# Order of two side jobs in one stage: unpacking of weights first, tables of heads 32 to 47 second

## The chip, the cores and the metric

One core of one Trainium2 chip. The metric is the device time of one execution in microseconds (us); the shown time of the kernel before is the median of three runs. The core's engines are TensorE (PE, matmuls, and PEld, its weight loads), VectorE (DVE), ScalarE (ACT), GpSimd (POOL) and SyncE (SP, which here only issues DMAs). Each engine works through its own instructions strictly in program order and waits on semaphores for the others.

## The reference

```python
def _L0_cond_ref(u, length, log_dt, C, log_A_real, A_imag, D):
    mask = (jnp.arange(Lq) < length[:, None]).astype(u.dtype)
    u_m = u * mask[:, None, :]
    kernel = _get_kernel(log_dt, C, log_A_real, A_imag, Lq)      # [64 heads, 1024]
    k_f, u_f = jnp.fft.rfft(kernel, n=2 * Lq), jnp.fft.rfft(u_m, n=2 * Lq)
    y = jnp.fft.irfft(u_f * k_f, n=2 * Lq)[..., :Lq] + u_m * D[:, None]
    return y * mask[:, None, :]

def _L0_ffn_ref(x, ...):
    x2 = x.reshape(-1, H).astype(jnp.float32)
    Wg, Wu, Wd = (dequant_gptq(...) for gate, up, down)          # 4-bit weights, groups of 128 rows
    gate, up = x2 @ Wg, x2 @ Wu
    inter = gate * jax.nn.sigmoid(gate) * up
    return (inter @ Wd).astype(jnp.float16).reshape(B, S, H)

x = x + _L0_ffn_ref(_L0_cond_ref(x, ...), ...)                   # x: (32, 64, 1024) float32
```

A long convolution of length 1024 for each of 64 heads (its kernel is made from the parameters of a state space model), then a gated feed-forward layer of 1024 by 2752 with packed 4-bit weights, then the residual sum. The 32 x 64 rows of `x` are the tokens.

## The kernel before

The 2048 tokens are worked on as four blocks of 512: block b holds the heads 16b to 16b+15, for all 32 batch entries. Activations are held as a high and a low float16 half (`xh`, `xl`, `ihl`), so each product is two matmuls.

The convolution of a head (`conv_head`) multiplies by Toeplitz tiles. To get them, a head's kernel is first computed from tables: `head_coefficients`, a decay table (Exp on ACT, L179), phase tables (`phase_tables`: L192 to L204 on DVE, Sin and Square on ACT, L207 and L209), and two factors (`kernel_factors`, L218 to L223 on DVE). `make_kernel` multiplies the factors on PE (L427), splits the result (L431, L433) and writes it to DRAM (`kpad`, L435); `toeplitz` (L529) reads it back as a 128 x 2 x 1024 tile.

A weight piece is made by the generator `unpack`, in three steps that lie apart in the program: SP issues two loads (packed bytes, L582, and zero points, L583); after a pause DVE shifts and masks the nibbles in place (L588) and POOL adds the zero points in two or fewer cuts (L594); after another pause DVE subtracts 64 and turns bytes into fp8, cut by cut (L603). `drain` runs the 34 pieces in order, each beginning its loads while an earlier one is worked on: 22 pieces of the gate and up weights (`gu`, in tiles `w` and `wmix`), then 12 of the down weights (`dn`, tiles `wd`, three parts for each of four pairs of output tiles).

The feed-forward layer runs in chains. A chain (`gu_one`, `gu_pair`, `dn_pair`) accumulates in PSUM over the groups of 128 input rows. Since each group has its own scale, the accumulator is rescaled after every group by the ratio of neighbouring scales: by DVE (L622, one instruction for 128 x 1024 values) or by ACT (L624), whichever a plan of the engines' times says is done earlier. Up to three chains are in flight, so that PE works on two while the third is rescaled. Four matmuls make one group of one chain.

The function `roll` orders all this. Its items come in stages: 0 and 1 (first four weight tiles for block 0 and for block 1, each alone), 2 (**the two-block stage**: the other gate and up tiles, blocks 0 and 1 together, 35 chains; two extra items make the kernels of heads 32 to 39 and 40 to 47), 3 and 4 (down, blocks 0 and 1), 5 (gate and up for blocks 2 and 3), 6 and 7 (down, blocks 2 and 3). After each step of a chain `roll` serves the side jobs of the current stage in the order of their list in `sides`. Each job earns credit at its rate; a job with `None` in third place spends all its credit, one generator step for each unit, but only while `c.room()` holds, that is, while the plan has DVE no more than 1200 ns and ACT no more than 1500 ns behind PE. A step that gives DVE work moves that plan on, and so can close the room to the job behind it in the list.

What isn't ready in time is forced: `need`, called where a chain begins (and at groups 0, 8 and 16 of a down chain), runs the unpacking, pauses left out, until the piece is there; `kernel_item` does the same with `third`, the generator of the tables of heads 32 to 47. The tile framework then fixes the instruction order of each engine.

Stage 3 has as side jobs the unpacking, the tables and kernels of heads 48 to 63 (`fourth`) and the convolutions of blocks 2 and 3 (`convs`).

Of the kernel before, what the change touches and what calls it, by code (L numbers as in the profile page):

```python
# [32 lines left out]
RATES = {"first": (0.5, 4.6), "fill": (1.0, 0.8), "third": 0.5, "late": 0.5, "convs": 1.9}  # L33
# [819 lines left out]
def tile_ssm_ffn(ctx, tc, io):  # L853
# [4 lines left out]
    def drain(gens):  # L858
        for u, ahead in zip(gens, gens[2:] + [None, None]):
            for n, _ in enumerate(u):  # L860
                if n == 1 and ahead is not None:
                    next(ahead)
                yield

    unpacks = [c.unpack_gu(i) for i in (*range(NI - 1), NI, NI - 1)] + [Later(c.unpack_dn, k, part) for part in range(3) for k in range(4)]
    unpack_it = c.unpacking = drain(unpacks)
# [123 lines left out]
    def third():  # L990
        tiles = [c.cv.tile([128, 2, L], F16, name="t0", bufs=3) for _ in range(3)]
        small = [c.cv.tile([128, 8, 4, B], F16, name=k) for k in ("uh", "ul", "uh", "ul")]
        take = c.scratch(tiles[:2])
        c.prm = take([128, 5, H], F32)
        nc.sync.dma_start(c.prm, io["prm"])
        for _ in range(4):
            yield
        coefficients = head_coefficients(nc, nc.vector, co, take, c.prm, c.cst[:, 66:67], 32, 32)
        while True:
            with c.after("dve"), c.after("act"):  # L1000
                if next(coefficients, "end") == "end":
                    break
            c.dve(1000)
            yield
        yield from c.decays(c.scratch(tiles[2:]), (32, 40))
        c.small = ScratchPool(c.scratch(small))
        c.taps(c.small, 32)
        for h0 in (32, 40):
            yield from c.tables(ScratchPool(c.scratch(tiles[:2])), h0, 8)
            yield from c.factors(c.small, h0, 8, c.xds[h0])  # L1010

    third_it = third()
# [37 lines left out]
    def residuals():  # L1050
# [7 lines left out]
    sides = {  # L1058
        0: [(unpack_it, RATES["first"][0], None), (group_it, 1.0, None), (second_it, RATES["first"][1], True)],
        1: [(unpack_it, RATES["fill"][0], None), (third_it, RATES["fill"][1], None)],  # L1060
        2: [(third_it, RATES["third"], None), (unpack_it, RATES["fill"][0], None)],
        3: [(unpack_it, RATES["fill"][0], None), (fourth_it, RATES["late"], False), (convs_it, RATES["convs"], False)],
        4: [(fourth_it, RATES["fill"][1], None), (convs_it, RATES["convs"], True)],
        6: [(residuals(), 1.0, True)],
# [80 lines left out]
```

## Time and profile before

| what | value |
|---|---|
| median of three runs | 1068.9 us (1068.55 to 1068.94) |
| profiled execution, its own time | 1069.55 us |
| its span in the profile | 1067.8 us |
| PE busy | 1019.1 us, 95% |
| DVE busy | 804.4 us, 75% |
| ACT busy | 777.6 us, 73% |
| POOL busy | 248.4 us, 23% |
| mean granted PE clock | 0.993 |
| first matmul of the two-block stage, of the down stage of block 0, of stage 5 | about 138, 395 and 572 us |

The span is the time from the first to the last instruction of the profiled execution; the execution's own time is a little longer. A line of a group in the profile names source line, engine, operation, output and inputs, shape and count, then the busy time and the mean of one in ns, then how long the engine sat idle before such instructions and what ended that. In a timeline each line has start and length in us, and in brackets the idle time of that engine just before, with the instruction that ended it; equal instructions that follow each other are merged (x2). A row of windows has, after its length, busy time and number of instructions for PE, PEld, DVE, ACT and POOL, then the granted PE clock, the DMA share and GB/s. Matmuls overlap in the pipeline, so a matmul of 0.38 us can follow the one before after 0.22 us.

### The profile page before, as it was taken

Reading aid. Unit: us, or ns where it says so; the run is one execution under the profiler, and the core shown is the slowest. Engines: PE = TensorE matmul, PEld = TensorE weight load, DVE = VectorE, ACT = ScalarE, POOL = GpSimd, SP = SyncE. Lnnn points to the kernel's source line nnn. Section 1 sums busy time; section 2 is a strip of 40 time slices with the busy share of each in tenths; the row PEclk is TensorE's granted clock in tenths of the full one; section 3 lists DMA queues with packets and bytes.
Section 4 is the critical chain, followed back from the end, with each engine's and each line's share of the span. In section 5 each row is a group of like instructions: output and inputs, shape, how many; then the busy total and the mean of one; then the engine's idle time right before and its main releaser. Section 6 shows DMA issues by size and latency. Waiting matters only on the chain.

```text
span 1067.8 us, 15316 instructions
## 1 busy us (share of the span) xinstructions
PE 1019.1 (95%) x5824; PEld 508.8 (48%) x5824; DVE 804.4 (75%) x924; ACT 777.6 (73%) x1033; POOL 248.4 (23%) x270
## 2 busy tenths in 40 slices
PE   2979999999899999999999999999999999999996
PEld 2857444444344445555565444444444444444442
DVE  8765788888987787886556767777787777777776
ACT  4867678787677778777777776666666667778775
POOL 0433133232332352223012102222211122102102
PEclk9989999999999999999999999999999999999999
DMA  6976321111011422568663001000000002424002
GB/s 203 316 238 216 107 79 40 40 60 40 32 57 51 140 91 104 165 178 273 183 206 119 30 20 39 21 21 20 12 20 21 20 21 61 147 80 155 33 1 79
DMA packets 52066, 99.74 MB, mean 93 GB/s; under 512 B 9492, under 2 KB 11412, under 8 KB 51992
## 3 DMA queue, kind: packets, MB, share of 16 engines
q1 hardware_dynamic: 38888, 70.09, 20.6%
q0 software_dynamic: 5280, 17.31, 4.3%
q10 hardware_dynamic: 7824, 11.37, 3.7%
q8 instruction: 45, 0.74, 0.3%
q14 instruction: 29, 0.24, 0.1%
HBM read 78.99 MB, written 19.76 MB: 92 GB/s over the span
## 4 chain that ended last, share of the span: by engine, by line
PE 80%; DVE 9%; ACT 4%; issue 3%; DMA 2%; POOL 1%; DVEq 0%; SPq 0%; ACTq 0%; POOLq 0%
PE chq L691 22%; PE chq L692 22%; PE chq L746 13%; PE chq L747 12%; PE cq L552 6%; PE chq L669 2%; PE chq L668 2%; DVE chq L622 1%; DMA t<-kpad 1%; ACT chq L624 1%; DVE v L704 1%; ACT chq L644 1%; DVE chq L641 1%; ACT sg L699 1%; PE chq L751 1%
## 5 line engine op out<-in xcount | busy, mean ns | idle before, releaser
L691 PE MATMUL chq<-xh,w 128*128 128x512 f16 x1216 | 459.6, 379 | 7.3 <-DVE chq L622 2.1
L692 PE MATMUL chq<-xl,w 128*128 128x512 f16 x1216 | 457.0, 379 | 0.0
L622 DVE TENSOR_SCALAR chq<-chq,gur 128x1024 f32<-128x1024 f32 x261 | 332.5, 1289 | 96.0 <-PE chq L692 95.4
L624 ACT ACTIVATE chq<-chq,gur 128x1024 f32<-128x1024 f32 x285 | 303.7, 1085 | 89.0 <-PE chq L692 88.4
L644 ACT ACTIVATE chq<-chq,dnr 128x512 f32<-128x512 f32 x374 | 242.7, 661 | 74.3 <-PE chq L747 68.1
L746 PE MATMUL chq<-ihl,wd 128*128 128x512 f16 x672 | 253.7, 379 | 2.2 <-DVE wd L603 0.8
L747 PE MATMUL chq<-ihl,wd 128*128 128x512 f16 x672 | 253.2, 379 | 0.0
L641 DVE TENSOR_TENSOR chq<-chq,dnr 128x1024 f32<-128x1024 f32 x128 | 156.5, 1231 | 77.5 <-PE chq L747 77.0
L692 PEld LDWEIGHTS <-w 128*128 128x128 fp8e4 x1216 | 118.5, 97 | 155.8 <-issue 20.4
L691 PEld LDWEIGHTS <-w 128*128 128x128 fp8e4 x1216 | 118.3, 97 | 147.9 <-issue 2.0
L310 POOL TENSOR_TENSOR ihl<-v,ihl 128x512 f16<-128x512 f32 x42 | 48.3, 1149 | 344.4 <-ACT ihl L633 344.4
L747 PEld LDWEIGHTS <-wd 128*128 128x128 fp8e4 x672 | 65.5, 97 | 71.2 <-issue 6.2
L746 PEld LDWEIGHTS <-wd 128*128 128x128 fp8e4 x672 | 65.4, 97 | 69.1 <-DVE wd L603 2.0
L552 PEld LDWEIGHTS <-t 128*128 128x128 f16 x1152 | 81.4, 98 | 34.2 <-DMA t<-kpad 1.3
L552 PE MATMUL cq<-uh,t 128*128 128x256 f16 (+3 forms) x720 | 91.3, 228 | 0.4 <-DMA t<-kpad 0.4
L552 PE MATMUL cq<-ul,t 128*128 128x256 f16 (+3 forms) x360 | 72.2, 228 | 0.0
L569 POOL TENSOR_TENSOR xl<-y,xh 128x512 f16<-128x512 f32 x28 | 36.4, 1298 | 145.1 <-ACT xh L567 142.7
L633 ACT CAST ihl<-v 128x512 f16<-128x512 f32 x42 | 25.9, 616 | 56.5 <-DVE v L704 53.1
L704 DVE SCALAR_TENSOR_TENSOR v<-chq,gul,sg 128x1024 f32<-128x1024 f32 x38 | 48.6, 1280 | 16.7 <-PE chq L692 7.9
L668 PE MATMUL chq<-xh,w 128*128 128x512 f16 x128 | 48.8, 384 | 4.5 <-ACT xh L567 3.1
L644 ACT ACTIVATE chq<-chq,gur 128x512 f32<-128x512 f32 x66 | 43.2, 660 | 13.6 <-PE chq L669 12.4
L310 POOL TENSOR_TENSOR spill<-v,spill 128x512 f16<-128x512 f32 x42 | 48.7, 1160 | 14.3 <-ACT spill L633 14.3
(258 smaller groups left out, 799.0 us busy)
## 6 DMA issues: line engine op xcount, KB each, us to landing
t<-kpad SPq DMA_DIRECT2D x48, 512.0 KB, 4.8
spill<-spill POOLq DMA_DIRECT2D x42, 256.0 KB, 2.3
ihl<-spill ACTq DMA_DIRECT2D x42, 256.0 KB, 2.7
z<-zc SPq DMA_DIRECT2D x29, 256.0 KB, 4.2
u<-xF SPq DMA_DIRECT2D x12, 512.0 KB, 4.4
xr<-xT SPq DMA_DIRECT2D x12, 512.0 KB, 4.7
out<-xr POOLq DMA_DIRECT2D x24, 256.0 KB, 2.9
w<-qgu SPq DMA_DIRECT2D x21, 256.0 KB, 4.0
```

What stands on the lines that cost most here:

```text
L310: self.nc.gpsimd.tensor_tensor(out, a, b, op)
L552: nc.tensor.matmul(q[:, d:, h % 2, :], t0[:, lw, 128 * d:128 * d + 128], uu[:, 0:8 - d, h % 4, :], start=(d == 0 and k == 0 and h % 2 == 0 ...
L622: self.mark("dve", self.nc.vector.tensor_scalar(q, q, col, None, ALU.mult))
L624: self.mark("act", self.nc.scalar.activation(q, q, AF.Copy, scale=col))
L641: self.mark("dve", self.nc.vector.tensor_tensor(q, q, cols.to_broadcast([128, 2, 512]), ALU.mult))
L644: self.mark("act", self.nc.scalar.activation(q[:, k], q[:, k], AF.Copy, scale=cols[:, k]))
L668: nc.tensor.matmul(q[:, k], lw, xh[:, g, :], start=(g == 0), stop=False, skip_group_check=True)
L691: nc.tensor.matmul(q[:, b], lw, xh[:, g, :], start=(g == 0), stop=False, skip_group_check=True)
L692: nc.tensor.matmul(q[:, b], lw, xl[:, g, :], start=False, stop=(g == GH - 1), skip_group_check=True)
L704: nc.vector.scalar_tensor_tensor(v, q, last, self.sg.pop(ct - 21), ALU.mult, ALU.mult)
L746: nc.tensor.matmul(qs[j], lw, self.ihl[:, g, 0], start=(g == 0), stop=False, skip_group_check=True)
L747: nc.tensor.matmul(qs[j], lw, self.ihl[:, g, 1], start=False, stop=False, skip_group_check=True)
```

## The change

In the two-block stage the list of side jobs is turned round. `unpack_it` is served first at every step, at its rate of 1.0, and `third_it` second, at its rate of 0.5; before it was the other way. Rates, conditions and all other stages stay.

```diff
@@ sides @@
         1: [(unpack_it, RATES["fill"][0], None), (third_it, RATES["fill"][1], None)],
-        2: [(third_it, RATES["third"], None), (unpack_it, RATES["fill"][0], None)],
+        2: [(unpack_it, RATES["fill"][0], None), (third_it, RATES["third"], None)],
         3: [(unpack_it, RATES["fill"][0], None), (fourth_it, RATES["late"], False), (convs_it, RATES["convs"], False)],
```

In the built program this moves the unpacking of all later pieces forward: the last L603 of weight tile 12, for example, stands 93 matmuls ahead of its first use before and 239 after, and the loads of the last down piece are issued in the two-block stage. The tables move back: the decay table from matmul place 1345 to 1562, the first factors' end from 1576 to 1866, the second's from 1732 to 2093. Places count PE's matmuls in program order; the two-block stage has the places 1038 to 2182, block 0's down stage begins at 2183. The numbers of matmuls and of unpacking steps are the same in both; the plan, which sees another order, also gives a few rescales to the other engine (of the two-block stage's L622 two fewer, of its L624 two more).

## The prediction

> **What bounds the kernel now.** I read the page first. TensorE (PE) is busy for 95% of the span and holds 80% of the chain of work that ended last; VectorE (DVE) and ScalarE (ACT) are busy for three quarters each, mostly with the rescales that stand between two matmul groups of one chain.
>
> ```profile
> PE 1019.1 (95%) x5824; PEld 508.8 (48%) x5824; DVE 804.4 (75%) x924; ACT 777.6 (73%) x1033; POOL 248.4 (23%) x270
> PE 80%; DVE 9%; ACT 4%; issue 3%; DMA 2%; POOL 1%; DVEq 0%; SPq 0%; ACTq 0%; POOLq 0%
> L622 DVE TENSOR_SCALAR chq<-chq,gur 128x1024 f32<-128x1024 f32 x261 | 332.5, 1289 | 96.0 <-PE chq L692 95.4
> ```
>
> Only waits of PE count, then. Next, the windows by stage: the two-block stage ends at about 395 us, the first down stage at about 490, the second at about 572.
>
> ```profile
> 195.00:395.00 200.00, 195.12 (x913) 86.00 (x911) 164.07 (x174) 151.70 (x164) 63.98 (x71) 1.00 0.21 67
> 395.00:490.00 95.00, 91.58 (x699) 53.09 (x697) 79.83 (x100) 73.07 (x114) 29.91 (x35) 1.00 0.49 155
> 490.00:572.00 82.00, 81.99 (x655) 49.96 (x654) 42.33 (x41) 63.68 (x101) 15.60 (x16) 1.00 0.65 204
> ```
>
> The columns are length, then PE, weight loads, DVE, ACT, POOL, clock and DMA. PE's clock is 1.00, so nothing here is the clock. PE's worst stretch is in the timeline of PE, and beside it that of DVE:
>
> ```profile
> 282.99 0.38 PE L692 MATMUL chq<-xl,w 128*128 128x512 f16 x1
> 284.89 0.38 PE L691 MATMUL chq<-xh,w 128*128 128x512 f16 x1 [1.52 <-DVE chq L622]
> ...
> 286.18 0.38 PE L691 MATMUL chq<-xh,w 128*128 128x512 f16 x1 [0.48 <-issue]
> ...
> 287.78 0.38 PE L691 MATMUL chq<-xh,w 128*128 128x512 f16 x1 [0.58 <-DVE w L603]
> ...
> 291.50 0.39 PE L691 MATMUL chq<-xh,w 128*128 128x512 f16 x1 [0.29 <-DVE w L603]
> ```
>
> ```profile
> 284.75 2.89 DVE L603 TENSOR_SCALAR w<-w 128x1024 fp8e4<-128x1024 uint8 x2
> 287.56 1.28 DVE L622 TENSOR_SCALAR chq<-chq,gur 128x1024 f32<-128x1024 f32 x1
> 288.75 0.86 DVE L588 TENSOR_SCALAR w<-w,cst 128x1024 uint16<-128x1024 uint16 x2
> 290.24 2.34 DVE L603 TENSOR_SCALAR w<-w 128x1024 fp8e4<-128x1024 uint8 x2 [0.62 <-POOL w L594]
> ```
>
> The weights of tiles 14 and 15 are unpacked at the last moment: DVE makes them (L588, L603) while PE stands before their first matmul, and the rescales (L622) queue behind. The down stage has the same picture:
>
> ```profile
> 471.15 0.39 PE L746 MATMUL chq<-ihl,wd 128*128 128x512 f16 x1 [0.63 <-DVE wd L603]
> ```
>
> ```profile
> 483.67 0.59 PE L751 MATMUL chq<-ic,wd 128*128 128x512 f16 x2 [1.31 <-DVE chq L641]
> ```
>
> **The measure of a loss.** Undisturbed wide matmuls start 0.216 us apart (282.78, then 282.99). What a start is later than that is lost to PE for good. I call matmuls by their place in PE's program order. First uses stand within 26 places of each other in the two programs, so places stand for time. A rescale that has waited starts 0.42 us after its last matmul's start, so 0.2 after that matmul's slot (the hop below); back to back on DVE it takes 1.2 of its 1.29 us, L603 0.6 of 0.68.
>
> **That the order does change.** In the built programs the last L603 of tile 13 stands 2 matmuls ahead of its first use before, 224 after; tile 14: 1 and 242; tile 15: 6 and 230; tile 17: 3 and 235. The down pieces that stood 2, 1, 8 ahead of, or behind, their use stand 379 to 452 ahead. From L603's 0.68 us and the loads' 3.7 to 4.9 us of landing, 200 matmuls (43 us) hide any of them. Nothing differs after place 3525 (572 us).
>
> **Removed in the two-block stage.** Losses at 259.24 (0.49), 284.89 (1.68), 286.18 (0.64), 287.78 (0.75), 291.50 (0.45), 293.83 (0.16) and 318.54 (0.15): 4.3 us, all at a first use or behind such a burst on DVE. Bounds: 2.5 (the 1.68 stays, as a rescale can be late for other reasons) to 4.3. I take 4.3, since in the new order no unpacking stands next to a first use.
>
> **Removed in the down stage.** Directly behind L603: 439.64 (0.32), 457.87 (0.26), 464.38 (0.31), 471.15 (0.79): 1.7. Behind DVE's queue: 442.84 (0.35), 469.93 (0.26), 483.67 (1.48): 2.1. Nine L603, five L588 and ten POOL adds (L594) leave this stage; the queue before 483.67 is a residual add (1.65 us), table work and a split, which partly stay. I take 1.0 of the 2.1. Sum 2.7, bounds 1.7 to 3.8.
>
> **Added to the two-block stage.** Those nine L603 and five L588: 9 x 0.683 + 5 x 0.475 = 8.5 us of DVE. Cover: DVE sits idle for 200 - 164 = 36 us of the window. Their weight loads (5 more there) go out on SP ahead of the three Toeplitz loads (L529), which land in 4.8 us and are first used at place 2207, 100 matmuls (21 us) behind. Without that cover a load would cost its 4.8 us. Where the cover is thin, I add up places:
>
> - The decay table's Exp moves from place 1345 to 1562, and the next Silu stands at 1572: two table loads around one Exp. From place 1540 ACT and DVE owe: 0.2 hop, Silu 1.1, product on DVE 1.2, two casts 1.2, a rescale 1.1, load 1.28, Exp 1.06, load 1.28, Silu 1.1 = 9.5 us. PE needs that bank at place 1579, 39 x 0.216 = 8.4 us on. So 1.1 late; the old Silu load's loss at 225.39 (0.32) goes. Net +0.8, bounds -0.3 (all hidden, as the old Exp's load at 208.31 was) and +1.6.
>
> ```profile
> 208.31 1.28 ACT L179 ACT_TABLE_LOAD   x1
> 222.93 1.28 ACT L699 ACT_TABLE_LOAD   x1
> ```
>
> - The factors of heads 40 to 47 (L218 to L223), formerly ended at place 1732, now end at 2093, three places ahead of the matmuls (2096) that read them: `kernel_item` had to force them. From place 2074 DVE owes: hop and product 1.4; then a rescale that waits for PE 2081 (1.73), done at 3.2, while PE wants it at 2086 (2.6): 0.6 late; L218 and L219 0.35 each and a rescale 1.2, done at 5.1, wanted at 4.1: 1.0 late; L222, L603, L223 1.4, done at 6.5, wanted at 6.4: 0.1. Together 1.7; the trace of before loses 0.3 there. Net +1.4. What waits behind is all of PE. Bounds 0 and 3.3 (five factor steps at 0.42 by their rows, 2.1, and a whole rescale, 1.2, all uncovered).
> - The phase tables of heads 32 to 39 cost 1.37 before (229.72 to 241.50: 0.23, 0.25, 0.56, 0.33), those of 40 to 47 0.1. Now L603, L588, L194, L197, L198 and a rescale queue at places 1685 to 1709: 5.2 to 6.0 us against 5.2, some 0.7 late; the second set, at places 1952 to 1970, some 0.5 by the same count. Net -0.3, bounds -1.5 (all hidden) to +0.7 (both 1.1). L194 ranges widely by its row:
>
> ```profile
> L194 DVE TENSOR_TENSOR t<-wl,cst x2: 681/1060/1439, 229.6 to 262.8; 128x512 f32<-128x512 f32 x2
> L603 DVE TENSOR_SCALAR w<-w x36: 679/683/1639, 72.5 to 357.3; 128x1024 fp8e4<-128x1024 uint8 x36
> ```
>
> - Places 2000 to 2105: by the rows' durations DVE owes 22.7 us there, against 17.0 before and PE's 21.4. Overlap of back-to-back instructions hides some, waiting for PE adds some. Beyond the second bullet I take +0.8, the middle of 0 and 1.5 (a little over 22.7 - 21.4).
>
> Two rules of the Trainium skill speak against the change. "ScalarE: Activation LUTs", section "Table sets: the hidden batching unit", wants functions of one set batched and gives about 2.7 us for a load; this trace has 1.283 us each time, and the trace decides. By the page's figure the first bullet would be 2.8 us dearer. "SBUF — State Buffer", section "Who interferes with whom", says that VectorE instructions with two SBUF inputs and some single-input ones block against GpSimd; the two rows above (0.68 to 1.44, 0.68 to 1.64) are as if it were so. If three more of them met L594, the sum by this rule would lose some 2.5 us of DVE time, most of it under the idle 36.
>
> **The sum.** -4.3 - 2.7 + 0.8 + 1.4 - 0.3 + 0.8 = -4.3 us. The profiled span of 1067.8 (its own time 1069.55, 0.65 above the median of 1068.9) becomes 1063.5; the median becomes 1064.6. With the terms' nearer bounds the likeliest case runs from 1062.3 to 1066.7.
>
> **Rivals.**
>
> - The moved work is nearly free. For it: DVE's 36 idle us, and that the planner gives rescales to ACT when DVE is full. Against it: the factors stand directly before their matmuls. All of 4.3 + 3.8 gone, 0.9 lost: -7.2, 1061.7. Chance 0.15.
> - The stall moves. The high bounds 1.6 + 3.3 + 0.7 + 1.5 = 7.1 give back the 7.0. For it: PE waits in order, so the factors and the Exp block all three chains. Against it: each high bound needs the worst overlap. 1069.0, no change. Chance 0.17.
> - Slower: DVE becomes the bound of the two-block stage from place 1565 to 2105. The 8.5 us come on top in full, only the down stage's 2.7 are won: +5.8, 1074.7. It decides once DVE's work exceeds PE's pace over long stretches and not only over the last 105 places. Against it: by rows the stretches between 1571 and 2000 hold 12 to 14.5 us of DVE against PE's 13.8 per 64 places. Chance 0.07.
> - That the edit does nothing is excluded by the order told above.
>
> **Numbers.** The forecast has 0.61. Two times apart by less than 0.2% (2.1 us: 1066.8 to 1071.0) cannot be told from no change here. Faster: 0.15 and nearly all of 0.61, 0.74; the same: 0.18; slower: 0.08. The range, 1061.6 to 1068.6, takes in most of the forecast, of the first rival and half of the second.
>
> **What would show it.** Right: no PE wait on L603 between 195 and 490 us; PE's waits by DVE near 440 to 484 us mostly gone; two table loads within 4 us near 256, with a wait of about 1 us behind them; a wait near 372 us on L622 and L223. Wrong: DVE above 95% busy in the second half of the stage, or PE waiting more than 3 us before the matmuls of L427 at place 2096, or fresh waits of ACT's rescales around the tables' Sin and Square.

## The result, and the profile after

| | before | after |
|---|---|---|
| median | 1070.04 us (1068.55 to 1072.18, 11 runs) | 1073.45 us (1071.24 to 1076.07, 11 runs) |
| ratio | 1 | 1.0034, 95% interval 1.0025 to 1.0043 |
| span of the profiled execution | 1067.8 us | 1073.2 us |
| PE's places 1038 to 2182, two-block stage | 257.0 us | 265.6 us |
| places 2183 to 2862, first down stage | 94.8 us | 91.9 us |
| before place 1038; from place 2863 on | 138.3; 577.7 us | 137.8; 577.9 us |

The kernel became 0.34% slower (3.4 us), where 0.4% faster (4.3 us) was forecast. The forecast was made from the first three of the eleven runs of before, whose median is 1068.9 us. The down stage gains 2.9 us, about what was forecast; the two-block stage loses 8.6 us. The page of after, as far as it answers to the lines of before:

```profile
PE 1019.6 (95%) x5824; PEld 511.1 (48%) x5824; DVE 809.4 (75%) x925; ACT 775.9 (72%) x1029; POOL 247.2 (23%) x270
PE 79%; DVE 11%; ACT 4%; issue 3%; DMA 2%; POOL 0%; DVEq 0%; SPq 0%; ACTq 0%
L622 DVE TENSOR_SCALAR chq<-chq,gur 128x1024 f32<-128x1024 f32 x259 | 330.6, 1290 | 91.8 <-PE chq L692 90.4
```

DVE's busy time rises by 5.0 us with one instruction more, and its share of the chain of work that ended last from 9 to 11%. The windows of after, for the two-block stage and the two down stages (columns as in the prediction):

```profile
138.00:403.00 265.00, 251.53 (x1162) 111.59 (x1161) 223.19 (x278) 197.93 (x217) 89.22 (x102) 0.99 0.21 67
403.00:495.00 92.00, 90.72 (x695) 53.10 (x693) 73.50 (x89) 69.67 (x107) 22.15 (x25) 1.00 0.43 139
495.00:578.00 83.00, 82.92 (x671) 50.74 (x671) 42.26 (x41) 64.23 (x102) 16.00 (x15) 1.00 0.64 206
```

DVE is busy for 223 of 265 us: 84%, so it isn't the bound over the stage. It is late at single places. PE's losses by place (start to start, less the pitch of an undisturbed matmul, us), summed from the two traces (a sum can be off by 0.1 to 0.2, and in the last row by more, with the pitch that is taken):

| places | before | after | what is lost there after |
|---|---|---|---|
| 1038 to 1189 | 2.6 | 4.0 | 1.71 at place 1080 (before 0.33): ACT waits for the landing of a store |
| 1190 to 1339 | 0.8 | 2.8 | 1.13 and 1.16 at 1196 and 1334: stretched table steps and L603, L588 ahead of a rescale |
| 1340 to 1559 | 2.2 | 1.6 | the phase tables' four losses are gone, 0.54 is new |
| 1560 to 1589 | 0.5 | 1.8 | 1.33 behind the Exp between two table loads |
| 1590 to 1719 | 4.1 | 1.0 | the forced weights' losses are gone |
| 1720 to 1859 | 0.7 | 2.6 | 0.92, 0.73, 0.32, 0.32 from 1828 to 1852 |
| 1860 to 1989 | 1.0 | 2.1 | 1.29 at 1957 |
| 1990 to 2065 | 0.0 | 0.2 | |
| 2066 to 2105 | 0.3 | 4.9 | the factors of heads 40 to 47 |
| 2106 to 2183 | 0.5 | 0.1 | |
| 2184 to 2862 | 6.9 | 3.8 | the late down pieces are gone |

Place 1080 is no work of the change: instructions stand alike there, and e2 below, which has after's order up to there, loses 0.41. What differs is how long the store takes from issue to landing: 2.58 us in before, 2.65 in e2, 3.96 in after, and 3.94 in the trace of e5, which loses 1.69 there.

**The dearest place.** The timelines of after, first PE, then DVE, then POOL:

```profile
382.78 0.44 PE L691 MATMUL chq<-xh,wmix 128*128 128x512 f16 x1 [2.51 <-DVE chq L622]
383.01 0.63 PE L691 MATMUL chq<-xh,w 128*128 128x512 f16 x1
383.43 0.63 PE L692 MATMUL chq<-xl,w 128*128 128x512 f16 x1
```

```profile
377.90 1.29 DVE L622 TENSOR_SCALAR chq<-chq,gur 128x1024 f32<-128x1024 f32 x1 [0.28 <-PE chq L692]
379.10 1.13 DVE L218 SCALAR_TENSOR_TENSOR ul<-t,t 128x256 f32<-128x256 f32 x1
380.15 1.37 DVE L219 SCALAR_TENSOR_TENSOR uh<-t,ab 128x256 f32<-128x256 f32 x1
381.44 1.28 DVE L622 TENSOR_SCALAR chq<-chq,gur 128x1024 f32<-128x1024 f32 x1
```

```profile
378.79 1.16 POOL L310 TENSOR_TENSOR ihl<-v,ihl 128x512 f16<-128x512 f32 x1 [1.36 <-ACT ihl L633]
379.91 1.33 POOL L310 TENSOR_TENSOR spill<-v,spill 128x512 f16<-128x512 f32 x1
```

PE stands for 2.51 us until the rescale of 381.44 is done. Two factor steps stand before that rescale. They take 1.13 and 1.37 us, where 0.41 and 0.42 are usual (the row of e6 below), and for just that time POOL makes the low halves of the products (L310, a subtraction with both inputs in SBUF). Then the matmuls start 0.43 us apart, not 0.216. The windows of after at this place show why:

```profile
380.00:382.00 2.00, 0.27 (x2) 0.00 (x0) 2.00 (x3) 1.09 (x1) 1.70 (x2) 1.00 0.00 0
382.00:384.00 2.00, 1.22 (x4) 0.53 (x4) 2.00 (x5) 0.00 (x0) 0.10 (x1) 0.74 0.36 135
384.00:386.00 2.00, 2.00 (x18) 0.89 (x17) 0.59 (x1) 0.98 (x1) 0.00 (x0) 0.50 0.72 219
386.00:388.00 2.00, 2.00 (x17) 1.09 (x15) 0.45 (x2) 1.54 (x4) 0.00 (x0) 0.91 0.92 225
```

The granted clock (last column but two) fell to 0.50, by the records from 382.96 to 386.38 us. The stall so costs some 1.3 us more after its end.

**The same in small** at 316 to 323 us: PE, DVE and POOL of after.

```profile
320.78 0.38 PE L691 MATMUL chq<-xh,w 128*128 128x512 f16 x1 [0.75 <-DVE chq L622]
...
322.37 0.38 PE L691 MATMUL chq<-xh,w 128*128 128x512 f16 x1 [0.56 <-DVE chq L622]
```

```profile
316.63 2.89 DVE L603 TENSOR_SCALAR wd<-wd 128x1024 fp8e4<-128x1024 uint8 x2
319.45 1.28 DVE L622 TENSOR_SCALAR chq<-chq,gur 128x1024 f32<-128x1024 f32 x1
```

```profile
316.27 1.15 POOL L310 TENSOR_TENSOR ihl<-v,ihl 128x512 f16<-128x512 f32 x1 [2.15 <-ACT ihl L633]
317.38 1.60 POOL L310 TENSOR_TENSOR spill<-v,spill 128x512 f16<-128x512 f32 x1
```

Two L603 that usually need 1.3 us back to back take 2.89 beside POOL, and the rescale behind them starts 1.6 us late. Nothing was forced here; the piece has over 300 matmuls of slack. The rows by line over the whole of after (shortest, median, longest in ns) tell which instructions stretch and which never do:

```profile
L603 DVE TENSOR_SCALAR wd<-wd x24: 411/684/1641, 316.6 to 452.9; 128x1024 fp8e4<-128x1024 uint8 x20, 128x512 fp8e4<-128x512 uint8 x4
L588 DVE TENSOR_SCALAR wd<-wd,cst x12: 406/477/1374, 307.2 to 423.9; 128x1024 uint16<-128x1024 uint16 x8, 128x768 uint16<-128x768 uint16 x4
L622 DVE TENSOR_SCALAR chq<-chq,gur x259: 1277/1293/1295, 141.6 to 917.0; 128x1024 f32<-128x1024 f32 x130
```

The rescales (PSUM in, PSUM out) take the same time throughout this trace. What lies in SBUF stretches, in these two rows up to threefold. Counted over DVE's instructions of the two-block stage that are over 150 ns above the shortest of their shape, the stretch is 11.4 us in 19 instructions before and 18.7 us in 31 after: 7.3 us more, made of 6.4 more beside the adds of the unpacking (L594), 2.3 more beside L310 and 1.4 less beside POOL's products for the decay table (L175). In the down stage it falls from 6.5 to 3.2 us.

### The profile page after: what moved, and what is told of

The parts are those of the page before. It is cut to its first block, busy times and chain, and to the rows that moved or that the text cites. A ratio compares the mean times of both kernels' runs of the same rounds, so it can differ in the third digit from the quotient of the medians.

```text
span 1073.2 us, 15317 instructions
## 1 busy us (share of the span) xinstructions
PE 1019.6 (95%) x5824; PEld 511.1 (48%) x5824; DVE 809.4 (75%) x925; ACT 775.9 (72%) x1029; POOL 247.2 (23%) x270
## 4 chain that ended last, share of the span: by engine, by line
PE 79%; DVE 11%; ACT 4%; issue 3%; DMA 2%; POOL 0%; DVEq 0%; SPq 0%; ACTq 0%
PE chq L691 21%; PE chq L692 20%; PE chq L746 13%; PE chq L747 13%; PE cq L552 6%; DVE chq L622 3%; PE chq L669 2%; PE chq L668 2%; DMA t<-kpad 1%; ACT chq L624 1%; ACT chq L644 1%; DVE v L704 1%; ACT sg L699 1%; PE chq L751 1%; DVE w L603 0%
## 5 line engine op out<-in xcount | busy, mean ns | idle before, releaser
L691 PE MATMUL chq<-xh,w 128*128 128x512 f16 x1216 | 459.2, 379 | 12.1 <-DVE chq L622 6.2
L692 PE MATMUL chq<-xl,w 128*128 128x512 f16 x1216 | 457.4, 379 | 0.0
L622 DVE TENSOR_SCALAR chq<-chq,gur 128x1024 f32<-128x1024 f32 x259 | 330.6, 1290 | 91.8 <-PE chq L692 90.4
L624 ACT ACTIVATE chq<-chq,gur 128x1024 f32<-128x1024 f32 x287 | 305.7, 1085 | 91.5 <-PE chq L692 91.2
L644 ACT ACTIVATE chq<-chq,dnr 128x512 f32<-128x512 f32 x368 | 239.3, 661 | 74.8 <-PE chq L747 68.8
L641 DVE TENSOR_TENSOR chq<-chq,dnr 128x1024 f32<-128x1024 f32 x131 | 160.4, 1231 | 81.4 <-PE chq L747 80.7
L692 PEld LDWEIGHTS <-w 128*128 128x128 fp8e4 x1216 | 118.8, 98 | 163.6 <-issue 28.4
L691 PEld LDWEIGHTS <-w 128*128 128x128 fp8e4 x1216 | 118.8, 98 | 146.5 <-issue 3.6
L310 POOL TENSOR_TENSOR ihl<-v,ihl 128x512 f16<-128x512 f32 x42 | 48.3, 1150 | 307.0 <-ACT ihl L633 307.0
L310 POOL TENSOR_TENSOR spill<-v,spill 128x512 f16<-128x512 f32 x42 | 49.4, 1177 | 15.7 <-ACT spill L633 15.7
```

The source lines that it names most:

```text
L310: self.nc.gpsimd.tensor_tensor(out, a, b, op)
L622: self.mark("dve", self.nc.vector.tensor_scalar(q, q, col, None, ALU.mult))
L624: self.mark("act", self.nc.scalar.activation(q, q, AF.Copy, scale=col))
L641: self.mark("dve", self.nc.vector.tensor_tensor(q, q, cols.to_broadcast([128, 2, 512]), ALU.mult))
L644: self.mark("act", self.nc.scalar.activation(q[:, k], q[:, k], AF.Copy, scale=cols[:, k]))
L691: nc.tensor.matmul(q[:, b], lw, xh[:, g, :], start=(g == 0), stop=False, skip_group_check=True)
```

## The experiments

In the expectations these theories stand by letters. J: the factors are made just in time, and the stalls are those of work that comes too late. P: work of DVE in SBUF is stretched beside POOL's, and the rescales queue behind it. L: the 8.5 us of unpacking that moved into the stage are too much for DVE. C: the half clock behind PE's idle time is a large part of the loss.

**e1, the tables at full rate.** In after, the tables' credit doubled:

```diff
-RATES = {"first": (0.5, 4.6), "fill": (1.0, 0.8), "third": 0.5, "late": 0.5, "convs": 1.9}
+RATES = {"first": (0.5, 4.6), "fill": (1.0, 0.8), "third": 1.0, "late": 0.5, "convs": 1.9}
```

> The changed kernel with the tables' rate at 1.0 in place of 0.5: weights still first, but the factors of heads 40 to 47 end at place 1973, 109 ahead of their matmuls, and are not forced. Theory J (the just-in-time factors at places 2066 to 2105 cost most: 4.9 us lost there in the changed kernel's trace, with 3.4 us of half clock, against 0.3 before): that loss falls below 1 us, and the time is 4 to 5 us below the changed kernel, 1068.5 to 1069.5, no slower than before. Theory P (side work on DVE is stretched beside POOL's subtractions and adds, 18.7 us in the two-block stage against 11.4, and rescales queue behind it): the stretch stays at 16 us or more, single losses of 1 us stay, the time is 1070 to 1072. Theory L (8.5 us more DVE work in the stage is what costs): no better than the changed kernel, 1072 to 1074.

Measured: 1071.51 us, ratio to before 1.0013 (1.0003 to 1.0022), span 1068.6. The last factors now end at place 1973, and places 2066 to 2105 lose 0.3 us. Larger losses stand elsewhere: 2.08 at 1593, 2.20 at 1708 (0.53 in after), 1.16 at 1842; the 1.28 at 1957 stays as in after. In time is not enough; DVE's stretch in the stage is 19.2 us. The 2.20 at 1708 is only in part stretch. There DVE stands still, with a rescale behind, until POOL has done the add that an L603 needs:

```profile
292.29 1.20 DVE L603 TENSOR_SCALAR w<-w 128x1024 fp8e4<-128x1024 uint8 x1 [1.46 <-POOL w L594]
```

In after no instruction of DVE in this stage waits so for POOL behind 144.4 us. The time, 1071.5, is as theory P had it; theory J's part, the loss at the factors, went as it said and didn't bring the time.

**e2, the kernels of heads 40 to 47 two chains later.** In after:

```diff
-            for at, h0 in ((33, 40), (29, 32)):
+            for at, h0 in ((35, 40), (29, 32)):
```

> The changed kernel with the item that makes the kernels of heads 40 to 47 two chains later in the list: its matmuls stand at place 2178 and the factors end at 2110, 68 places ahead. All other orders stay. Theory J: the loss of 4.9 us at places 2066 to 2105 goes, PE's clock stays at 1.00, time 1068.5 to 1069.5. Theory P: losses of 1 us elsewhere stay; as the L218 and L219 stand beside POOL's subtractions still, 1 us of the 4.9 stays: 1070 to 1071. Theory L: 1072 or more.

Measured: 1069.61 us, ratio 0.9997 (0.9988 to 1.0006): before's time. Places 2066 to 2105 lose 0.25 us, all other losses of after stay to within 0.2 us (1.12 and 0.97 at 1196 and 1334, 1.33 at 1576, 2.3 from 1828 to 1852, 1.29 at 1957), save that of place 1080. Two losses are new, 0.59 and 0.42 at 2107 and 2118. The 1 us that theory P left at the factors didn't stay. The windows of e2 around the place:

```profile
372.00:382.00 10.00, 9.92 (x47) 4.39 (x46) 9.02 (x11) 7.34 (x9) 4.83 (x6) 1.00 0.19 67
382.00:400.00 18.00, 17.32 (x94) 7.95 (x93) 15.85 (x18) 12.63 (x14) 6.82 (x8) 1.00 0.28 85
```

DVE is as full as in after (224.2 us busy between 138 and 399 us, where after has 223.2 between 138 and 403), and the clock stays at 1.00. So this one place is worth 1073.45 - 1069.61 = 3.8 us of after's median, more than the 3.4 by which after is slower. And the rest of the change together is worth nothing: its gains pay for its other losses.

**e3 and e9, the weights of the two-block stage first, then the tables, the down pieces last.** In after, the job is split in two:

```diff
+    def gu_part():
+        while ("gu", NI - 1) not in c.ready:
+            next(unpack_it)
+            yield
+    def dn_part():
+        while True:
+            if ("gu", NI - 1) in c.ready:
+                next(unpack_it, None)
+            yield
-        2: [(unpack_it, RATES["fill"][0], None), (third_it, RATES["third"], None)],
+        2: [(gu_part(), RATES["fill"][0], None), (third_it, RATES["third"], None), (dn_part(), RATES["fill"][0], None)],
```

> Unpacking first only until the last gate and up tile is ready, then tables first, then the down pieces, which so mostly go back to the down stage, as before. Theory L: the two-block stage gets its DVE load back, and the time is below before: 1065 to 1067. Theory P: about as many stretches up to place 1700, fewer behind; kernel 40's factors end 62 places ahead: 1068 to 1070, with the down stage's 2.7 us lost again. Theory J: 1068 to 1069, as the factors are not at the last moment.

> The order of the earlier run (gate and up weights first, down pieces last) once more with more rounds: theories J and P both leave it 1 to 2 us faster than before, 1068 to 1069 against 1070; theory L has nothing against it. If it is the same as before within 0.1%, none of the orders wins anything.

Measured: 1068.79, ratio 0.9988 (0.9979 to 0.9998), and again 1069.26, ratio 1.0000 (0.9991 to 1.0009). The first interval ended just below 1, and the repeat gave the gain back: no difference from before. DVE's stretch was 14.9 us, between before and after.

**e4, the tables first but slow.** In before, `"third": 0.5` became `"third": 0.25`.

> The kernel before (tables first) with the tables' rate at 0.25 in place of 0.5; weights of tiles 13, 15 and 16 are still forced, the factors end 230 places ahead of their matmuls. If the forced weights cost what I took for them (4.3 us), they still do: 1068 to 1070. If the spread of table work over the stage is what helps (fewer steps together in front of a rescale), 1066 to 1068.

Measured: 1076.84, ratio 1.0068 (1.0053 to 1.0083), the slowest of all; neither expectation came true. The largest losses are 3.03 us at place 1700, PE waiting for an L603, and 2.75 at 1808 to 1815. At the first, PE, DVE, POOL and the windows of e4:

```profile
291.12 0.39 PE L691 MATMUL chq<-xh,w 128*128 128x512 f16 x1 [2.86 <-DVE w L603]
```

```profile
286.25 0.61 DVE L588 TENSOR_SCALAR w<-w,cst 128x1024 uint16<-128x1024 uint16 x1
288.35 2.11 DVE L588 TENSOR_SCALAR w<-w,cst 128x1024 uint16<-128x1024 uint16 x1
290.38 1.81 DVE L603 TENSOR_SCALAR w<-w 128x1024 fp8e4<-128x1024 uint8 x2
```

```profile
286.55 1.33 POOL L310 TENSOR_TENSOR spill<-v,spill 128x512 f16<-128x512 f32 x1
288.76 1.41 POOL L594 TENSOR_TENSOR w<-w,z 128x256 int32<-128x256 int32 x2
```

```profile
289.00:292.00 3.00, 0.88 (x5) 0.41 (x6) 3.00 (x3) 0.45 (x1) 2.62 (x4) 1.00 0.38 139
292.00:296.00 4.00, 4.00 (x12) 1.50 (x11) 1.98 (x3) 2.75 (x3) 0.77 (x1) 0.57 0.45 153
```

The half clock followed here too. The weights are late, and POOL makes them later: the L588 at 286.25 is done at 286.86, but the next adds (L594) begin at 288.76, behind POOL's subtraction and the issue of a store; and the L603 that PE waits for stand behind a second L588 that takes 2.11 us beside these adds, where 0.48 is usual. Of the 2.75 us, 0.64 and 0.74 (places 1811 and 1815) come with two L603 that take 2.89 us beside L310. DVE's stretch in the whole stage is 12.4 us, near the 11.4 of before: the sum says little, the place of a stretched step decides.

**e5, PE kept busy through the wait.** In after, 20 matmuls of 128 x 256 into unused columns of the bank, ahead of the factors' own:

```diff
+        if h0 == 40:
+            for n in range(20):
+                nc.tensor.matmul(kq[:, 0, 256:512], self.w[:, 19, 0, n % 8, :], self.x[0][0][:, n % 8, :256], start=True, stop=True,
+                                 skip_group_check=True)
```

> The changed kernel with 20 extra matmuls of 128 x 256 on ready operands (their result is written over) ahead of the matmuls of heads 40 to 47, to keep PE at work while the factors are made. Theory C (PE's clock halves for 3.4 us because PE stood idle for about 2.7 us): no half clock near 383 us, and though PE gets 20 x 0.11 = 2.2 us more work, the time is not above the changed kernel's: 1071.5 to 1073.5. Rival (the half clock has nothing to do with the idle time): the half clock stays near 383 us, and the time is up to 2 us above the changed kernel: 1073.5 to 1075.5.

Measured: 1074.51, ratio 1.0043 (1.0028 to 1.0058), and the clock was halved at 383.0 all the same. The fill didn't fill: PE went on waiting and lost 1.97 us at place 2104 behind the 20 matmuls (idle for 1.80), and the 3.41 us before the drop still had PE busy for only 47%. So it says nothing on what the half clock costs, and theory C was not tested by it.

**e6, after without POOL's subtraction.** L310 becomes a constant fill, so the low half of the gate and up products is left out:

```diff
-        self.pool_first(hl[:, 1], v, hl[:, 0], ALU.subtract)
+        with self.tc.high_priority(offset=300):
+            self.nc.gpsimd.memset(hl[:, 1], 0.0)
```

**e7, before with the same edit.**

> The changed kernel with POOL's subtraction (the low half of the products, L310) replaced by a write of zeros, so the low half of the gate and up products is left out. POOL then neither reads two tiles nor holds 1.15 us each. Theory P (side work on DVE is stretched beside POOL and rescales queue behind it): the 8.6 us of stretch beside L310 falls to 2 us or less, the wait before the matmuls of heads 40 to 47 falls below 2 us without half clock, and the time falls by 5 to 8 us to 1066 to 1068.5; against its partner without the change (next run) it is no more than 1 us slower. Rival (the order alone, each instruction at its usual duration): it stays 3 us slower than its partner.

> The kernel before with the same replacement (the low half of the gate and up products is left out). Theory P: 6.3 us of stretch beside L310 go, 2 to 4 us of the waits at forced weights with them: 1066 to 1068. Rival: 1069 to 1070, as POOL is not on the path.

Measured: e6 1067.26, ratio to before 0.9975 (0.9966 to 0.9984); e7 1067.11, ratio 0.9979 (0.9970 to 0.9988). The two orders stand 0.15 us apart, where they were 3.4 apart. The places of after that lost 1.13, 0.54, 1.65 and 1.29 (1196, 1452, 1828 with 1832, 1957) lose 0.29, 0, 0 and 0 in e6 (though 0.83 stands at 1840, where after has 0.32); 1334 goes from 1.16 to 0.59, and places 2066 to 2105 lose 2.0 where after lost 4.9. The dearest place again, DVE and PE of e6 (the edit makes line numbers behind it one higher, so L692 here is after's L691):

```profile
371.60 1.29 DVE L622 TENSOR_SCALAR chq<-chq,gur 128x1024 f32<-128x1024 f32 x1 [0.39 <-PE chq L693]
372.80 0.41 DVE L218 SCALAR_TENSOR_TENSOR ul<-t,t 128x256 f32<-128x256 f32 x1
373.13 0.42 DVE L219 SCALAR_TENSOR_TENSOR uh<-t,ab 128x256 f32<-128x256 f32 x1
373.46 1.29 DVE L622 TENSOR_SCALAR chq<-chq,gur 128x1024 f32<-128x1024 f32 x1
```

```profile
372.94 0.38 PE L692 MATMUL chq<-xh,w 128*128 128x512 f16 x1 [0.52 <-DVE chq L622]
...
374.81 0.38 PE L692 MATMUL chq<-xh,wmix 128*128 128x512 f16 x1 [0.84 <-DVE chq L622]
```

DVE has the same instructions in the same order as in after, all 366 of the two-block and the first down stage: 0.66 us from the start of L218 to the rescale, against 2.34 in after. The wait that is left is 0.84 and the clock isn't halved. The edit also takes away POOL's own wait for the high half and some of its time, so the medians alone don't say that stretching did it; the rows of L218, L219 and L603 do, since they shrink where POOL's read is gone. The stretch beside L594 stays in e6 (8.5 us) and costs PE less: where it stands ahead of a rescale, 0.59 us at 1334 and 0.83 at 1840 (an L603 of 1.20 us).

**e8, the tables up to the decay table first, then the weights, then the rest of the tables at rate 1.0, the down pieces last.** In after (`third_part` runs `third_it` until the decay table exists, `third_rest` from there):

```diff
+        2: [(third_part(), RATES["third"], None), (gu_part(), RATES["fill"][0], None), (third_rest(), 1.0, None), (dn_part(), RATES["fill"][0], None)],
```

> A third order of the same side jobs: tables first up to the decay table, then gate and up weights first, then the other tables at rate 1.0, then the down pieces. No weights are forced (the nearest stands 40 matmuls ahead of its use), the two table loads stand 56 places apart, the factors end 287 places ahead of their matmuls. Theories J and P together: the losses of the changed kernel at places 1571 to 1579 (1.8 us) and 2066 to 2105 (4.9) go, those of the kernel before at forced weights (4.3 and 1.7) too, while stretches beside POOL leave 1 us here and there: 1065 to 1068, faster than both. Theory L: 1069 to 1071.

Measured: 1074.27, ratio 1.0049 (1.0036 to 1.0062). This falls: nothing is forced, no first use is nearer than 40 matmuls to its L603, and yet it is slower than after. The largest loss, 2.83 us, is at place 1196. DVE, POOL, then PE of e8 there:

```profile
173.29 3.60 DVE L108 TENSOR_SCALAR wh<-t 128x32 f32<-128x32 f32 x1
...
177.34 1.29 DVE L622 TENSOR_SCALAR chq<-chq,gur 128x1024 f32<-128x1024 f32 x1
```

```profile
173.45 1.41 POOL L594 TENSOR_TENSOR w<-w,z 128x256 int32<-128x256 int32 x2
174.81 2.03 POOL L175 TENSOR_TENSOR t<-na,cst 128x512 f32<-128x512 f32 x2
```

```profile
178.68 0.38 PE L691 MATMUL chq<-xh,w 128*128 128x512 f16 x1 [2.66 <-DVE chq L622]
```

An instruction on 32 columns that takes 0.17 us at 175.77 in after took 3.60: it ended when four instructions of POOL in a row were done. So being early is not enough; in this trace, as in after, the largest loss comes of a step beside POOL's work directly ahead of a rescale.

**e10 and e11, less of it on DVE.** ACT takes the final unpacking step (L603) of the weight tiles 8, 10, ..., 20, in e10 with the edit of e2, in e11 with that of e3:

```diff
-                               act=i < 3)
+                               act=i < 3 or i % 2 == 0 and i > 7)
```

> The run with the matmuls of heads 40 to 47 two chains later (weights first throughout), and besides the last step of the unpacking of tiles 8, 10, 12, 14, 16, 18 and 20 (12 to 14 of the L603) on ACT in place of DVE, where the trace of before has 1.14 us each. Theory P: those steps cannot be stretched beside POOL any more, and the losses of 1 us behind them go; but ACT gets some 14 x 1.1 = 15 us more, beside some 12 us less on DVE. 1066 to 1069. Theory L (total work of DVE counts): 1064 to 1066. If ACT's queue takes DVE's place as what the rescales wait in: 1070 to 1073.

> Gate and up weights first, down pieces last, and the last unpacking step of the even tiles from 8 on ACT. Theory P: below the same order without it, 1066 to 1068. If ACT's queue takes DVE's place: 1069 to 1072.

Measured: 1073.41, ratio 1.0035 (1.0023 to 1.0047), and 1071.70, ratio 1.0028 (1.0016 to 1.0040): 3.8 and 2.4 to 2.9 us slower than without it. The numbers lie near the third expectation, but its reason doesn't show in the traces: behind 138 us no single wait of PE on ACT is longer than 1.0 us. In both the largest loss of the two-block stage is 2.20 us at place 1717, and it is DVE's. DVE and PE of e10 (L624 is the rescale there):

```profile
289.68 1.39 DVE L588 TENSOR_SCALAR w<-w,cst 128x1024 uint16<-128x1024 uint16 x1
291.60 2.04 DVE L194 TENSOR_TENSOR t<-wl,cst 128x512 f32<-128x512 f32 x1
```

```profile
296.15 0.38 PE L693 MATMUL chq<-xh,w 128*128 128x512 f16 x1 [2.04 <-DVE chq L624]
```

L588 and L194 stand beside L310 and L594 of POOL; their shortest times are 0.47 and 0.68. The steps that went to ACT are no longer stretched, others are: e10's stretch in the stage is 18.8 us, where e2's is 18.1. By places e11's two-block stage is 2.9 us longer than e3's. That of e10 is as long as e2's, and e10's trace loses 2.6 us (e2 0.7) far behind it, at place 3841, where DVE waits for the landing of a store. Why e10's median is 3.8 us above e2's stays open.

No order tried beats before by what can be measured. What stays open is how much the half clock is worth by itself, and how an order would look that keeps SBUF work of DVE away from POOL's subtractions and adds by design: that was not tried.

## Why the prediction was wrong

By its own terms (us; minus is a gain):

| term | predicted | measured |
|---|---|---|
| forced weights, two-block stage | -4.3 | -3.8; in the place of the 0.49 at 259.24, one of 0.48 stands one place on |
| down stage | -2.7 | -2.9 |
| Exp between two table loads | +0.8 | +1.3 |
| factors of heads 40 to 47 | +1.4 | +4.6 |
| phase tables | -0.3 | +0.4: 0.53 and 1.29 for 1.37 and 0.1; the 1.29 stands behind a stretched L603 and L588 and is gone in e6 |
| places 2000 to 2065, the rest | +0.8 | +0.2 |
| not in the sum: places 1196, 1334, 1452, 1828 to 1852 | 0 | +5.1 |
| place 1080, a landing | 0 | +1.4 |

The right-hand column adds up to 6.3 us, the spans differ by 5.4; smaller losses that went make up the rest. They are single executions, and the last row differs from one to the next: the medians differ by 3.4. Of after's eleven runs the four with a mean clock of 0.993 took 1071.2 to 1072.0 us, the seven with 0.986 to 0.992 took 1072.7 to 1076.1, as if not every run met the half clock.

- **The order and the gains were right.** PE no longer waits for an L603 in the two-block stage, and PE's waits by DVE near 440 to 484 us went, as said. But e7 shows that the loss at forced weights was itself in part stretch: places 1590 to 1719 lose 4.1 us in before and 2.95 without POOL's subtraction.
- **Right in kind and nearly in size: the Exp.** Two loads of 1.28 us stand around it, and 1.1 late was worked out where 1.33 was lost. The 0.32 at 225.39, which should have gone with the old Silu load, stayed (0.35 at place 1424): it had another cause. ACT and PE of after:

```profile
259.45 1.28 ACT L179 ACT_TABLE_LOAD   x1
260.74 1.06 ACT L179 ACTIVATE t<-t 128x1024 f32<-128x1024 f32 x1
261.82 1.28 ACT L699 ACT_TABLE_LOAD   x1
263.11 1.11 ACT L699 ACTIVATE sg<-chq,gul 128x1024 f32<-128x1024 f32 x1
```

```profile
264.22 0.38 PE L691 MATMUL chq<-xh,w 128*128 128x512 f16 x1 [1.17 <-DVE chq L622]
```

- **The step that failed first: the factors.** The hand count (0.6 + 1.0 + 0.1 = 1.7) took L218 and L219 at 0.35 each. In e6, without stretch, the place loses 0.69 + 1.0 + 0.12 and some tenths, the count to the letter. In after it loses 0.68 + 2.67 and the half clock behind it, net +4.6 where +1.4 was in the sum. Even the high bound, 3.3, was worked out from undisturbed durations and was too low. The mechanism was right, and its size was set by what POOL does at the same time. PE's two waits there, 0.52 and 2.51 us, are just over the 3 us that the prediction had named as a sign of being wrong.
- **The step that failed most: the price of the side work.** The rule of the Trainium skill, "SBUF — State Buffer", section "Who interferes with whom", was weighed at 2.5 us of DVE time, "most of it under the idle 36". So it stood at nothing in the sum, and places 1196, 1334, 1452 and 1828 to 1852 lost 5.1 us. The stage's stretch rose by 7.3 us, and the idle time didn't cover it there: DVE is in order, and a rescale that PE wants stands right behind the stretched step. An engine's idle share over a stage says nothing of that. In e6 these places lose 2.0, so 3.1 of the 5.1 hang on POOL's subtraction.
- **Not the whole miss.** Without POOL's subtraction on either side (e6 against e7) the loss of 3.4 us is gone, but the gain of 4.3 isn't there either: the medians are equal. By places of the two traces e6 gains 2.1 at the forced weights (1590 to 1719) and 2.9 in the down stage, and gives back 1.3 at the Exp, 1.7 at the factors, 1.1 at 1720 to 1859 and 0.6 at 1190 to 1339. So the new order has deadlines of its own that cost about as much as the old ones, and the stretch beside L310 makes them dearer.
- **"Nothing here is the clock" held for before only.** It was read from before and carried over to a kernel with a longer stall.
- **Rivals.** "The stall moves" is the kind of what happened, with more given back than its bounds allowed. The slower case, DVE the bound by 8.5 us of load, isn't it: e6 carries the same load and is at e7's time, and e2 is at before's.

## What to carry to other kernels

Take a side instruction's cost from the longest of its row, not its median, if another engine's work can meet it, and ask what stands directly behind it in its engine's queue. Moving work earlier removes a stall at its first use, but the work then lies ahead of other deadlines: count the new neighbours, not only the slack. And one item placed a little later (e2) may be worth more than the order of all the side work.

## What the runs showed of the hardware

- **Stretch is selective.** The L622 rescales from PSUM to PSUM stay within 1277 to 1295 ns over 259 instructions of after (in e6 one shows 1615; its record begins 0.49 us before the stretched L108 ahead of it ends), while SBUF work beside POOL's two-input reads goes from 0.68 to 1.64 (L603), 0.48 to 1.37 (L588), 0.42 to 1.37 (L219), 0.17 to 3.60 (L108 in e8). Three single-input forms are among them (L603, L588, L108). The section of the Trainium skill named above counts some single-input forms in, and these rows agree.
- **The clock halves behind a stall that doesn't fill a window.** The drops in these stages last 3.41 us. The starts of all drops of a trace lie on a grid: in after, 24.56 and 382.96 us are 105 times 3.413 us apart. The step of the grid before a drop had PE busy for 26% (after), 34% (e4) and 47% (e5); no drop followed steps of 43% (e10), 44% (e1), 44% (e8) and 54% (before), so the share alone doesn't decide. Nor does the length of the wait: 2.66 us in e8, which two steps share, brought no drop, and 2.51 us in after, all in one step, did. The Trainium skill ("TensorE: Matmul & The Clock Gate", section "What's actually happening") puts the half clock behind an idle window of some 3.4 us. The length of the drops agrees; the condition does not, since PE's idle stretches ahead of the three drops were 1.8 to 2.9 us, and the measurement decides.
